# A graph attention layer: comparing edges with places and nodes on TensorE and ScalarE, loading sources by sixteens of rows, eight row buffers, and the 0/1 matrix and q in float32

## The chip, the cores and the metric

The kernel runs on one core of a Trainium2 chip. The metric is the device time of one execution in microseconds (us). Ten executions of the kernel before gave a median of 2691.25 us, from 2687.83 to 2693.83.

A core has five engines that run their own instruction streams side by side and wait for each other by semaphores: PE (TensorE, matmuls; its weight loads are listed as PEld), DVE (VectorE), ACT (ScalarE), POOL (GpSimd) and SP (SyncE, which here only issues transfers). Matmul results lie in PSUM, in banks of 128 partitions by 512 float32 columns; everything else lies in SBUF, 128 partitions wide.

## The reference

A graph of N = 12500 nodes with D = 128 features and M = 200000 edges that are sorted by their target node `dst`. Each node keeps the 16 best of its incoming edges, by a score, and adds the softmax-weighted messages of these to itself:

```python
h = relu(layernorm(x))
Qv, Ku = h @ W_Q.T, h @ W_K.T
score = einsum('md,md->m', Qv[dst], Ku[src]) / sqrt(128) * exp(-edge_weight)
keep  = rank of the edge by score among those of its dst < 16
w     = where(keep, exp(score - max over dst), 0)
alpha = w / (sum of w over dst)
agg   = segment_sum(alpha[:, None] * (h[src] @ W_msg.T), dst)
out   = x + relu(h @ W_self.T + agg)
```

Inputs and output are float32, indices int32.

## The kernel before

**Windows and chunks.** The edges are cut into chunks of 128 (one edge per partition), and 14 chunks (`GC`) make a window; there are G = 112 windows. A window's nodes are those whose edges begin in it, at most 128, one per partition; since the last of them can go on in the next window, a window works on 15 chunks (`NJ`), the fifteenth being the first of its neighbour.

**What is done for a window g**, by the names of the stages, with the engine and the line of the main instruction:

- `load_nodes`: SP loads the features of the nodes, `h_r` (from the table `h_tab` of normed rows, written in the setup) and `x_t`. `load_dst` (SP, L186): the targets of the window's 1920 edges, copied to all 128 partitions as int32, `dstb`, 960 KB.
- `let_go` (L464): DVE copies two chunks' source indices into `ix` (L472), and POOL issues an indirect gather for each of them (L172): 128 rows of `h_tab`, 64 KB, into `hs`. `hs` holds a window's 14 chunks and has seven buffers. 14 gathers a window.
- `h_turned`, `q_made`, `q_out`: the node rows transposed, and the queries q = hT times a_qk (W_Q and W_K in one matrix). `q_parts` (DVE, L516) splits the float32 q into three bfloat16 parts, whose sum is q.
- `far_of` (ACT, L522) and `to_edges` (ACT, L527): the 0/1 matrix of nodes by edges. Square of (dst minus the node's number) over 1920 columns, then Relu(1 - that): 1 where the edge belongs to the node, 0 elsewhere. Kept as bfloat16, `to_e`.
- `q_to_edges(g, b)` (PE, L546): each edge's own q, by a matmul of `to_e` with q, in four parts of four chunks, three matmuls a chunk (the three parts of q), into three banks of the tag "q". `scores` (DVE, L556): product with the gathered row, summed over the 128 features, and times the decay.
- `places` (DVE, L533 and L535): two more 0/1 matrices of 40 columns per chunk. `ow` says where in a strip of 40 nodes the edge's target stands (compared with `dlw`); `po` says the edge's place among its target's edges (compared with `pos_all`).
- `scores_in_slots` (DVE), `slots_by_node` (PE, L571, 15 matmuls into the bank "e"), `slots_out`, `node_by_slots`: the scores sorted into a matrix of nodes by 40 places.
- `best` (DVE, L585 to L597): the 16 best of 40, and `km`, which marks them. `sum_of_exps` (ACT, L602).
- `kept_to_edges` (PE, L614): the marks brought back to the edges, by `to_e`. `on_edges` (DVE, L620 to L627), `exps`, `weights` (DVE, L636): each edge's weight, laid out as a sparse matrix `alz`.
- `sums` (PE, L646, in two parts): `alz` times the gathered rows, summed over the 15 chunks in the one buffer of bank "a". `sums_out` (ACT, L651): times 1 over the sum, `agn`. After that `hs` of the window can be written again.
- `sums_turned`, `products`, `output`, `store`: the two weight matrices, relu, plus x, and the store.

**The order.** The loop (L684) is unrolled in full, as a software pipeline written by hand: iteration i runs each stage for another window, such as `q_to_edges` for i, `far_of` and `places` for i + 1, `slots_by_node` for i - 1, `best` and `kept_to_edges` for i - 2, `sums` for i - 3, `output` for i - 5, and `let_go` for i + 3 and i + 4 through `more(k)`. Each engine runs its instructions in the order of the program. Accesses to one PSUM bank wait for each other as whole banks: a new use of a bank with one buffer waits until its last reader is done.

**The setup** turns the index lists into columns: `src`, `dst` and the edge weights are loaded as 121 rows of 13 chunks (`RR`, `CPR`) on ACT's queue, and PE transposes them. `x` is loaded, normed and stored as `h_tab`. The first four windows (`RAW`) gather from `x` itself and are normed afterwards; the 42 gathers of windows 4 to 6 are issued together before the loop (`gather_at_once`). A general path behind a runtime flag follows the loop; it isn't taken here.

Of the kernel before, what the change touches and what calls it, by code (L numbers as in the profile page):

```python
# [20 lines left out]
P = 128  # L21
# [55 lines left out]
def gnn_layer(  # L77
# [38 lines left out]
    CPR = 13  # L116
# [4 lines left out]
    assert RR <= P and RR - RF <= 1  # L121
# [22 lines left out]
    nvec = const.tile([P, 1], F32, name="nvec")  # L144
    a_qk = const.tile([P, P], F32, name="a_qk")
    wselfT = const.tile([P, P], F32, name="wselfT")
    wmsgT = const.tile([P, P], F32, name="wmsgT")

    idx_all = const.tile([P, CW], I32, name="idx_all")
    dec_all = const.tile([P, CW], F32, name="dec_all")  # L150
    pos_all = const.tile([P, CW], F32, name="pos_all")
    dlw = const.tile([P, G, NJ], F32, name="dlw")

    nb = const.tile([P, G], F32, name="nb")
# [13 lines left out]
    def gather(g, j0, j1, index, table=h_tab):  # L168
        if j0 == 0:
            T[g]["hs"] = rows_pool.tile([P, GC, D], F32, name="hs", bufs=7)  # L170
# [8 lines left out]
    def load_dst(g):  # L179
        n = chunks[g] * P  # L180
        lo = g * EG
        T[g]["dstb"] = dstb = rows_pool.tile([P, NJ * P], I32, name="dstb", bufs=2)
        hi = min(lo + n, M)
        if hi < lo + n:
            nc.vector.memset(dstb[:, hi - lo:n], 1 << 21)
        nc.sync.dma_start(dstb[:, 0:hi - lo], dst[lo:hi].partition_broadcast(P))  # L186
# [47 lines left out]
    with tc.tile_pool(name="edges", bufs=1) as ep, ExitStack() as stage:  # L234
        prep = stage.enter_context(tc.tile_pool(name="prep", bufs=1))
        RL = HALO + RW

        src_r = ep.tile([RR, RL], I32, name="src_r")
        h0 = src_r.bitcast(F32)
        h1 = alz[0][0:RR, 0:RL]  # L240
        dst_all = alz[1][:, 0:CW]
        assert max(RL, CW) <= NJ * (WW + STEP)
        dst_r = ep.tile([RR, HALO + RW], I32, name="dst_r")
# [5 lines left out]

        def load_rows(t, a):  # L250
            if RF:
                nc.scalar.dma_start(t[0:RF, 0:RW], a[0:RF * RW].rearrange("(p c) -> p c", c=RW))
            if REM:
                nc.scalar.dma_start(t[RF:RF + 1, 0:REM], a[RF * RW:M].rearrange("(p c) -> p c", p=1))

        def to_columns(rows, lo, put):

            for j0 in range(0, CPR, 4):
# [5 lines left out]
                put(lambda t: t[:, 0:RR * CPR].rearrange("e (p j) -> e j p", j=CPR)[:, j0:j1, :],  # L264
# [3 lines left out]
        nc.vector.memset(src_r, 0)  # L268
        load_rows(src_r, src)
        xs, t = [], 0  # L270
        for i, n in enumerate(sizes):
            xg = prep.tile([HP, n, D], F32, name=f"xg{i}")
            for a, b in cuts:
                nc.sync.dma_start(xg[a:b], by_part(x)[a:b, t:t + n, :])
            xs.append((t, n, xg))
            t += n
        make_identity(nc, ident)
        nc.gpsimd.iota(dst_r, pattern=[[1, RL]], base=1 << 21, channel_multiplier=0)
        nc.gpsimd.memset(dst_r[0:1, 0:HALO], -1)
        nc.gpsimd.iota(slots, pattern=[[1, KM]], base=0, channel_multiplier=0,  # L280
# [3 lines left out]
        nc.vector.memset(ew_r, 0.0)  # L284
# [8 lines left out]
        nc.vector.memset(pos_all[:, RR * CPR:CW], 0.0)  # L293
        nc.vector.memset(dec_all[:, RR * CPR:CW], 0.0)
        nc.vector.memset(dst_all[:, RR * CPR:CW], float(1 << 21))
        for j in range(NJ):
            nc.vector.memset(w0[:, j:j + 1], float(lead(j)))
        for k in range(2):
# [6 lines left out]
        to_columns(src_f, 0, lambda at, p: nc.vector.tensor_copy(at(idx_all), p))  # L305
# [3 lines left out]
        def finish(i):  # L309
            t0, n, xg = xs[i]  # L310
            normed(xg, n, *stat[i])
            if i == 1:
                for t, w in zip(ws, (w_q, w_k, w_self, w_msg)):
                    nc.scalar.dma_start(t, w)
                nc.scalar.dma_start(b_i[:, 1:G],
                                    bass.AP(dst.tensor, dst.offset + EG - 1, [[EG, 1], [EG, G - 1]]))

                nc.scalar.dma_start(dst_r[0:1, HALO:], dst[0:RW].rearrange("(p c) -> p c", p=1))
                if RF > 1:
                    nc.scalar.dma_start(dst_r[1:RF, :], bass.AP(dst.tensor, dst.offset + RW - HALO,  # L320
                                                                [[RW, RF - 1], [1, RL]]))
# [608 lines left out]
```

## Time and profile before

| | |
|---|---|
| median of 10 runs | 2691.25 us (2687.83 to 2693.83) |
| the profiled execution | 2694.53 us |
| its span, first to last instruction | 2692.8 us |
| mean granted TensorE clock | 0.694 |
| setup, until the first `agn` | 215.1 us |
| last gather stream ends | about 2615 us |
| DMA moved | 253.17 MB, mean 94 GB/s |

Seen by stretches (busy us of each engine, instructions in brackets, the granted clock, the share of the DMA engines, and what they moved), the run is even from about 336 us on:

```profile
215.00:336.00 121.00, 75.50 (x666) 63.67 (x665) 73.66 (x337) 25.85 (x51) 72.76 (x70) 0.71 0.30 91
336.00:1000.00 664.00, 444.16 (x3772) 379.36 (x3772) 362.61 (x1860) 147.91 (x291) 389.67 (x406) 0.69 0.30 93
1000.00:2000.00 1000.00, 683.42 (x5686) 586.36 (x5686) 544.65 (x2786) 224.25 (x440) 587.72 (x612) 0.67 0.30 93
2600.00:2693.00 93.00, 60.38 (x626) 55.26 (x626) 54.52 (x265) 19.27 (x51) 13.34 (x13) 0.80 0.07 20
```

The order of the five engines is PE, PEld, DVE, ACT, POOL. A line of the profile such as `L646 PE MATMUL a<-hs,alz 128*128 128x128 f32 x1305 | 285.5, 386 | ...` is a group: line of the kernel, engine, operation, output and inputs by name, shapes, count, total busy us, mean ns of one, then the idle time of the engine just before these instructions and what ended it. A float32 matmul leaves two records. The ends of PE's records are modelled, and a wait whose releaser could not be found is called "remote".

### The profile page before, as it was taken

To read this page: it belongs to the slowest core of one execution; us is meant where nothing else is said; L and a number is where in the kernel's file an instruction comes from. 1 tells how busy PE (TensorE), PEld (TensorE's weight loads), DVE (VectorE), ACT (ScalarE), POOL (GpSimd) and SP (SyncE) were. 2 spreads that over 40 slices of the span, in tenths; PEclk is the share of its full clock that TensorE was granted. 3 is DMA by queue.
4 is the path that set the end of the run, shared out by engine and by line. 5 is a ranking of instruction groups with operands and counts; after the bars stand their busy time and mean duration, and the time that the engine had idled before them with its cause. 6 is when DMAs were issued, how large, how long until landed. Compare 5 with 4: busy or idle time off the path is not lost. (4 is left out here: it accounts for less than half of the span.)

```text
span 2692.8 us, 43581 instructions
## 1 busy us (share of the span) xinstructions
PE 1721.5 (64%) x14574; PEld 1474.3 (55%) x14575; DVE 1476.4 (55%) x7420; ACT 648.0 (24%) x1306; POOL 1522.1 (57%) x1578
## 2 busy tenths in 40 slices
PE   0226666666676666676666766666766666676676
PEld 0125555555565556565565655555655565555565
DVE  5447555555555555555555555555555555555555
ACT  5532122222222222222222222222222222222221
POOL 4734555555555555555555655555556555555540
PEclk9667666667767776766666666766677667766668
DMA  8412332333333333322332333233333333322320
GB/s 208 164 58 81 100 95 92 94 94 93 94 95 95 94 94 94 91 87 89 92 93 92 94 94 93 94 94 94 95 95 94 94 94 93 87 88 92 94 79 8
DMA packets 117573, 253.17 MB, mean 94 GB/s; under 512 B 32799, under 2 KB 76066, under 8 KB 116577
## 3 DMA queue, kind: packets, MB, share of 16 engines
q1 hardware_dynamic: 66104, 144.92, 15.5%
q0 software_dynamic: 50144, 102.74, 14.7%
q10 hardware_dynamic: 1094, 2.69, 0.5%
q8 instruction: 115, 1.88, 0.3%
q14 instruction: 116, 0.94, 0.1%
HBM read 236.40 MB, written 14.40 MB: 93 GB/s over the span
## 5 line engine op out<-in xcount | busy, mean ns | idle before, releaser
L172 POOL DMA_INDIRECT hs<-h_tab,ix x1465 | 1412.2, 964 | 1040.7 <-DVE prod L556 504.9
L646 PE MATMUL a<-hs,alz 128*128 128x128 f32 x3348 | 707.8, 377 | 98.9 <-issue 86.3
L546 PE MATMUL q<-q,to_e 128*128 128x128 bf16 x5022 | 546.1, 258 | 307.5 <-issue 257.9
L646 PEld LDWEIGHTS a<-hs,alz 128*128 128x128 f32 x3348 | 649.5, 283 | 147.3 <-issue 127.5
L546 PEld LDWEIGHTS <-to_e 128*128 128x128 bf16 x5022 | 418.2, 115 | 381.3 <-issue 368.9
L556 DVE SCALAR_TENSOR_TENSOR prod<-hs,dec_all,q 128x128 f32<-128x128 f32 x1674 | 483.7, 343 | 70.7 <-remote 53.9
L585 DVE TENSOR_SCALAR ell<-slots,e 128x40 f32<-128x40 f32 x112 | 27.9, 249 | 872.6 <-remote 841.3
L571 PE MATMUL e<-ow,sl 128*41 128x40 f32 x3348 | 250.8, 250 | 47.1 <-issue 45.3
L602 ACT ACTIVATE e<-v,km 128x16 f32<-128x16 f32 x112 | 34.4, 307 | 974.0 <-DVE km L594 964.9
L571 PEld LDWEIGHTS e<-ow,sl 128*41 128x41 f32 x3348 | 221.0, 166 | 71.9 <-issue 57.6
L654 PE MATMUL s<-ident,agn 128*128 128x128 f32 x112 | 40.4, 360 | 300.5 <-DVE o L666 99.2
L651 ACT ACTIVATE agn<-a,rden 128x128 f32<-128x128 f32 x112 | 41.1, 367 | 775.6 <-remote 550.7
L522 ACT ACTIVATE far<-dstb,nb 128x1920 bf16<-128x1920 int32 x112 | 213.0, 1901 | 0.0
L527 ACT ACTIVATE to_e<-far 128x1920 bf16<-128x1920 bf16 x112 | 201.1, 1796 | 0.0
L654 PEld LDWEIGHTS s<-ident,agn 128*128 128x128 f32 x112 | 17.5, 156 | 323.3 <-ACT agn L651 153.1
L556 DVE DVE_READ_ACCUMULATOR prod<-hs,dec_all,q 128x1 f32 x1674 | 138.0, 82 | 0.0
L472 DVE COPY ix<-idx_all 128x2 int32<-128x2 int32 (+1 forms) x733 | 130.6, 178 | 0.0
L666 DVE SCALAR_TENSOR_TENSOR o<-s,x_t 128x128 f32<-128x128 f32 x112 | 32.5, 290 | 126.0 <-issue 119.1
L614 PE MATMUL x<-km,to_e 128*128 128x43 bf16 x1674 | 78.8, 204 | 35.5 <-DVE km L597 30.9
L506 PE MATMUL s<-a_qk,hT 128*128 128x128 f32 x224 | 57.2, 337 | 68.0 <-ACT hT L503 57.8
L614 PEld LDWEIGHTS <-to_e 128*128 128x128 bf16 x1674 | 66.7, 112 | 58.9 <-DVE km L597 55.1
L564 DVE TENSOR_TENSOR sl<-po,s 128x600 f32<-128x600 f32 x112 | 87.6, 782 | 3.8
(166 smaller groups left out, 1639.3 us busy)
## 6 DMA issues: line engine op xcount, KB each, us to landing
dstb<-in_dst_dram SPq DMA_DIRECT2D x111, 960.0 KB
hs<-h_tab,ix POOLq DMA_INDIRECT x1465
h_r<-h_tab SPq DMA_DIRECT2D x112, 64.0 KB
x_t<-in_x_dram SPq DMA_DIRECT2D x108, 64.0 KB
out_dram<-o SPq DMA_DIRECT2D x108, 64.0 KB
xg<-in_x_dram SPq DMA_DIRECT2D x2, 1400.0 KB
h_tab<-xg SPq DMA_DIRECT2D x2, 1400.0 KB
xg<-in_x_dram SPq DMA_DIRECT2D x1, 1120.0 KB
```

The costliest lines, as they stand in the source:

```text
L172: nc.gpsimd.indirect_dma_start(out=T[g]["hs"][:, j, :], out_offset=None, in_=table[0:N, :], in_offset=bass.IndirectOffsetOnAxis(ap=index(j ...
L472: nc.vector.tensor_copy(ix[:, j0:j1], idx_all[:, GC * g + j0:GC * g + j1])
L506: nc.tensor.matmul(so[:, P:2 * P], lhsT=T[g]["hT"], rhs=a_qk, start=True, stop=True)
L522: nc.scalar.activation(T[g]["far"][:, 0:n], T[g]["dstb"][:, 0:n], AF.Square, bias=nb[:, g:g + 1])
L527: nc.scalar.activation(T[g]["to_e"][:, 0:n], T[g]["far"][:, 0:n], AF.Relu, bias=1.0, scale=-1.0)
L546: nc.tensor.matmul(pq[:, (j - j0) * P:(j - j0 + 1) * P], lhsT=T[g]["to_e"][:, j * P:(j + 1) * P], rhs=upper(T[g]["q"][:, k, :]), start=(k ...
L556: nc.vector.scalar_tensor_tensor(prod, rows_of(g, j), dec_all[:, c:c + 1], T[g]["pq", b][:, (j % 4) * P:(j % 4 + 1) * P], op0=OP.mult, op1 ...
L564: nc.vector.tensor_tensor(sl1[g % 2][:, 0:n, 0:KM], T[g]["po"][:, 0:n, :], bc(T[g]["s"][:, 0:n], KM), op=OP.mult)
L571: nc.tensor.matmul(et[0:KM + 1, STEP * j:STEP * j + WN], lhsT=sl1[g % 2][:, j, :], rhs=T[g]["ow"][:, j, :], start=False, stop=(j == n - 1))
L614: nc.tensor.matmul(px[:, j, 0:KM + 3], lhsT=T[g]["to_e"][:, j * P:(j + 1) * P], rhs=upper(T[g]["km"]), start=True, stop=True)
L646: nc.tensor.matmul(T[g]["pa"][:, 0:P], lhsT=alz[g % 2][:, WW * j + PRE:WW * j + PRE + P], rhs=rows_of(g, j), start=(j == 0), stop=(j == n ...
L654: nc.tensor.transpose(so[:, 2 * P:3 * P], T[g]["agn"], ident)
```

## The change

Five things are done together.

1. *Targets.* `load_dst` is gone. The setup keeps `rel`, 112 rows (one per window) of 1920 numbers in bfloat16: the edge's target minus the target of the edge just before the window's first, minus 1. `far_of` runs in four blocks of up to 512 edges: a matmul with a one-hot column copies the window's row of `rel` to all 128 partitions, in bank "a", and ACT squares it with the node's number subtracted.
2. *Places.* The two comparisons on DVE are gone. `edges_turned` transposes a window's 2 x 15 numbers per edge (`pd`: place and strip offset) by a matmul into bank "a", and ACT copies it to SBUF; `away`, three times, subtracts the 40 places by a matmul with the constant `minus_at`, 400 columns into bank "a", and ACT squares; `places` is one Relu(1 - that) over 1200 columns on ACT, giving `po` and `ow` in one tile.
3. *Float32.* `to_e` is float32, and q is used as it is: `q_parts` is gone, and `q_to_edges` makes one float32 matmul a chunk in place of three bfloat16 ones. `kept_to_edges` reads the upper halves of `to_e`.
4. *Gathers.* Eight `hs` buffers, seven `ix` buffers, and `more` lets go of windows i + 4 and i + 5; windows 4 to 6 are gathered by `let_go` too, the first of them in the setup and the others in the first iterations.
5. *Setup.* 112 rows of 14 chunks; the loads stand on SP's queue, and large ones are cut at a multiple of 16 rows.

Bank "a", with one buffer, now takes nine uses a window in place of one. In the order, `slots_by_node` is cut in three between the blocks of `far_of`, and `kept_to_edges` stands before the first part of `sums`. The core of the diff:

```diff
-            T[g]["hs"] = rows_pool.tile([P, GC, D], F32, name="hs", bufs=7)
+            T[g]["hs"] = rows_pool.tile([P, GC, D], F32, name="hs", bufs=8)
...
-    def load_dst(g):
-        n = chunks[g] * P
-        lo = g * EG
-        T[g]["dstb"] = dstb = rows_pool.tile([P, NJ * P], I32, name="dstb", bufs=2)
...
-        nc.sync.dma_start(dstb[:, 0:hi - lo], dst[lo:hi].partition_broadcast(P))
...
+        def sixteens(a, b):
+
+            m = b - (b - a) % 16
+            return [(p, q) for p, q in ((a, m), (m, b)) if p < q]
+
         def load_rows(t, a):
-            if RF:
-                nc.scalar.dma_start(t[0:RF, 0:RW], a[0:RF * RW].rearrange("(p c) -> p c", c=RW))
+            for p0, p1 in sixteens(0, RF):
+                nc.sync.dma_start(t[p0:p1, 0:RW], a[p0 * RW:p1 * RW].rearrange("(p c) -> p c", c=RW))
...
-        for g in range(RAW, min(7, G)):
-            gather_at_once(g, h_tab)
...
+        nc.vector.tensor_scalar(rel, dst_f[:, HALO:], dst_f[:, HALO - 1:HALO], 1.0, op0=OP.subtract, op1=OP.subtract)
...
-        def q_parts(g):
-
-            q = T[g]["q"]
-            for k in range(2):
-                nc.vector.tensor_sub(q[:, k + 1, :], q[:, k, :], upper(q[:, k, :]))
...
+        def far_of(g, b):
+            n0, n1 = 4 * P * b, min(4 * P * (b + 1), chunks[g] * P)
+            if n0 >= n1:
+                return
+            if b == 0:
+                T[g]["far"] = win.tile([P, NJ * P], BF16, name="far")
+            pr = bank("a", 1)
+            nc.tensor.matmul(pr[:, 0:n1 - n0], lhsT=upper(ident[0:RR, g:g + 1]).to_broadcast([RR, P]),
+                             rhs=rel[:, n0:n1], start=True, stop=True)
+            nc.scalar.activation(T[g]["far"][:, n0:n1], pr[:, 0:n1 - n0], AF.Square, bias=minus)
...
-            T[g]["to_e"] = win.tile([P, NJ * P], BF16, name="to_e", bufs=4)
+            T[g]["to_e"] = win.tile([P, NJ * P], F32, name="to_e", bufs=4)
...
+        def edges_turned(g):
+            pr = bank("a", 1)
+            nc.tensor.matmul(pr[0:32, 0:P], lhsT=pd[:, g, :, :].rearrange("e w j -> e (w j)"), rhs=upper(ident),
+                             start=True, stop=True)
+            T[g]["pdT"] = win.tile([32, P], BF16, name="pdT")
+            nc.scalar.copy(T[g]["pdT"], pr[0:32, 0:P])
+
+        def away(g, b):
+            if b == 0:
+                T[g]["aw"] = win.tile([P, 2 * NJ * KM], BF16, name="aw")
+            n0, n1 = 400 * b, 400 * b + 400
+            pr = bank("a", 1)
+            nc.tensor.matmul(pr[:, 0:400], lhsT=T[g]["pdT"],
+                             rhs=minus_at.rearrange("k w j s -> k (w j s)")[:, n0:n1], start=True, stop=True)
+            nc.scalar.activation(T[g]["aw"][:, n0:n1], pr[:, 0:400], AF.Square)
+
         def places(g):
...
+            T[g]["opo"] = win.tile([P, 2, NJ, KM], F32, name="opo", bufs=4)
+            nc.scalar.activation(T[g]["opo"].rearrange("e w j s -> e (w j s)"), T[g]["aw"], AF.Relu, bias=1.0,
+                                 scale=-1.0)
...
-                for k in range(3):
-                    nc.tensor.matmul(pq[:, (j - j0) * P:(j - j0 + 1) * P],
-                                     lhsT=T[g]["to_e"][:, j * P:(j + 1) * P], rhs=upper(T[g]["q"][:, k, :]),
-                                     start=(k == 0), stop=(k == 2))
+                nc.tensor.matmul(pq[:, (j - j0) * P:(j - j0 + 1) * P],
+                                 lhsT=T[g]["to_e"][:, j * P:(j + 1) * P], rhs=T[g]["q"], start=True, stop=True)
...
             def more(k):
 
-                g, k = (i + 3, k + 2) if k < 5 else (i + 4, k - 5)
-                if 7 <= g < G:
+                if i in (-1, 0, 1):
+                    g = i + 6
+                else:
+                    g, k = (i + 4, k + 2) if k < 5 else (i + 5, k - 5)
+                    if g < 8:
+                        return
+                if i >= -1 and g < G:
                     let_go(g, k)
 
             at(i, q_to_edges, 0)
+            at(i + 1, edges_turned)
             at(i - 5, output)
             at(i - 5, store)
             at(i - 3, weights)
             more(0)
             at(i - 4, sums_turned)
+            at(i + 1, far_of, 0)
             at(i - 4, sums_turned_out)
             at(i + 1, q_out)
             at(i, q_to_edges, 1)
-            at(i + 1, far_of)
-            at(i - 1, slots_by_node)
-            at(i + 1, places)
+            at(i + 1, far_of, 1)
+            at(i - 1, slots_by_node, 0)
+            at(i + 1, far_of, 2)
+            at(i - 1, slots_by_node, 1)
+            at(i + 1, far_of, 3)
+            at(i - 1, slots_by_node, 2)
+            at(i + 1, away, 0)
...
             at(i - 2, sum_of_exps)
             at(i - 1, slots_out)
             at(i, q_to_edges, 2)
+            at(i + 1, away, 1)
             at(i + 2, h_turned)
+            at(i + 1, away, 2)
             at(i, scores, 0)
             more(3)
             at(i + 1, to_edges)
-            at(i + 1, q_parts)
             at(i + 2, h_turned_out)
+            at(i - 2, kept_to_edges)
             at(i - 3, sums, 0)
-            at(i - 2, kept_to_edges)
...
             more(5)
+            at(i + 1, places)
```

## The prediction

> **What bounds the kernel now.** I read the engines' shares first, then the waits, then one window of the steady stretch in the timeline, then the durations by tile. No engine is full:
>
> ```profile
> PE 1721.5 (64%) x14574; PEld 1474.3 (55%) x14575; DVE 1476.4 (55%) x7420; ACT 648.0 (24%) x1306; POOL 1522.1 (57%) x1578
> ```
>
> so the bound is a loop of waits. The view of waits (engine, tile and line, what ended the wait: total us, times, longest) names it; about 110 windows are run:
>
> ```profile
> DVE ell L585 <- remote: 841.3, 98, 8.7
> ACT agn L651 <- remote: 550.7, 78, 7.3
> POOL hs L172 <- DVE prod L556: 504.9, 207, 54.7
> ...
> POOL hs L172 <- remote: 138.8, 84, 2.1
> ```
>
> "remote" is a releaser that the profile could not name. The timeline of one window (start, duration, instruction, idle before it) shows what it is:
>
> ```profile
> 1503.39 0.37 ACT L651 ACTIVATE agn<-a,rden 128x128 f32<-128x128 f32 x1 [7.03 <-remote]
> 1503.58 0.94 POOL L172 DMA_INDIRECT hs<-h_tab,ix  x1 [1.67 <-remote]
> 1504.11 0.84 PE L546 MATMUL q<-q,to_e 128*128 128x128 bf16 x12
> 1507.14 0.33 PE L571 MATMUL e<-ow,sl 128*41 128x40 f32 x4 [0.41 <-issue]
> 1512.53 0.94 POOL L172 DMA_INDIRECT hs<-h_tab,ix  x1 [0.30 <-issue]
> 1515.14 0.25 DVE L585 TENSOR_SCALAR ell<-slots,e 128x40 f32<-128x40 f32 x1 [8.65 <-remote]
> 1517.54 0.94 POOL L172 DMA_INDIRECT hs<-h_tab,ix  x1 [4.07 <-DVE prod L556]
> 1519.30 3.72 PE L646 MATMUL a<-hs,alz 128*128 128x128 f32 x16
> 1526.29 0.37 ACT L651 ACTIVATE agn<-a,rden 128x128 f32<-128x128 f32 x1 [7.11 <-PE q L546]
> 1526.48 0.94 POOL L172 DMA_INDIRECT hs<-h_tab,ix  x1 [1.74 <-remote]
> ```
>
> POOL issues a window's 14 gathers as a stream of eight (1503.58 to 1513.47) and one of six (1517.54 to 1524.74), one per 1.25 us within each. Alone that is 14 x 1.25 = 17.5 us. Between the streams stand gap A (4.07) and gap B (1.74), of which 0.3 each is the ordinary distance, so the period is 17.5 + 3.77 + 1.44 = 22.7; from agn to agn it is 22.9, and 22.83 over the 44 windows of 1000 to 2000 us. Gap A is POOL waiting for the index copies of DVE (L472), which stand behind ell. And ell waits for the slots matmuls L571, whose last record here ends at 1507.5, though DVE goes on only at 1515.14, 1.7 us after the last gather of the stream was issued. Gap B is the same with sums: the 16 matmuls of L646 end at 1523.0, agn starts at 1526.29 and frees POOL's next row buffer. I read this so: while gathers run one behind another, other engines see PE's results late, and what is still open is released when the stream ends. The end of the run supports it, where no gathers are left and agn follows every 11 to 13.5 us:
>
> ```profile
> 2619.48 0.37 ACT L651 ACTIVATE agn<-a,rden 128x128 f32<-128x128 f32 x1 [3.33 <-PE a L646]
> 2630.45 0.37 ACT L651 ACTIVATE agn<-a,rden 128x128 f32<-128x128 f32 x1 [1.68 <-PE a L646]
> ```
>
> So the time is 2694.53 us (this execution, span 2692.8) = 336 us of setup and ramp + 100 windows x 22.83 up to 2615 + a tail of about 80. The median of the runs, 2691.25, is 3 us lower.
>
> **The change, part by part.** Durations (lines of 1000 to 2000 us; total busy, mean ns):
>
> ```profile
> L546 PE MATMUL q<-q,to_e 128*128 128x128 bf16 x1968 | 217.9, 260 | 120.5 <-issue 102.7 <-DVE prod L556 16.9
> L522 ACT ACTIVATE far<-dstb,nb 128x1920 bf16<-128x1920 int32 x44 | 83.9, 1908 | 0.0
> L533 DVE TENSOR_TENSOR ow<-slots,dlw 128x600 f32<-128x600 f32 x44 | 33.9, 772 | 0.0
> L535 DVE TENSOR_TENSOR po<-slots,pos_all 128x600 f32<-128x600 f32 x44 | 33.9, 771 | 0.0
> L516 DVE TENSOR_TENSOR q<-q 128x128 f32<-128x128 f32 x88 | 25.4, 288 | 1.5
> L510 ACT COPY q<-s 128x128 f32<-128x128 f32 x44 | 12.0, 272 | 0.0
> ```
>
> *Taken off DVE:* places 772 + 771 and q_parts 2 x 288 = 2.1 us of a window's 12.2 (DVE's 544.65 us in those 1000, by 44.) Places lies at the start of the eight-stream, ahead of 8.65 us of waiting for ell; q_parts lies in the six-stream. Neither ends a gap: worth 0.
>
> *The dst broadcast,* 960 KB a window, goes; nothing waits for it (far starts with no idle time before it). Worth 0 by itself; the second rival prices what it may do to others.
>
> *far by blocks.* One Square of 1908 ns becomes four, each behind a matmul of 512 columns in bank a. From 272 ns at 128 columns to 1908 at 1920 the slope is 0.913 ns a column, so 512 columns take 272 + 384 x 0.913 = 620 ns. The matmul: twelve L546 records take 0.84 us at full clock and 1.49 at half in two neighbouring windows, some 57 and 107 ns per 128 columns, so 0.23 to 0.43 us. The hand-over PE to ACT outside a lag: aggT (L658) starts 0.66 us after its matmul ends (1503.98 + 0.30, 1504.94), which I halve between there and back: a turn costs about 0.62 + 0.35 + 0.35 = 1.3 us. The three away turns with 400 columns (520 ns) cost 1.2 each, the turned edges about 0.9, places' Relu of 1200 columns 272 + 1072 x 0.913 = 1.25 us. So ACT rises from 5.1 to some 9.2 us a window and PE's wide matmuls add 2 to 3.5 us; neither fills.
>
> What matters is the order. Bank a has one buffer, so edges_turned, four far blocks, three away blocks and the sums follow each other, PE to ACT to PE, and PE executes in order: the second part of slots stands behind far block 2, the third, whose end ell needs, behind block 3. In the eight-stream block 1 stands behind q(1)'s 8 f32 records, block 2 behind slots' first 10. If their signals come late as L571's do now, then when the stream ends PE has not yet been allowed to issue the rest. Left from there: none of the turns if all four get through in the stream (for that speaks aggT, released within 0.66 us inside a stream), at most all four, 4 x 1.3 = 5.2 us. I take one and a half turns, **1.95 us on gap A**, since two blocks stand behind ten or more f32 records each and only these. Queued behind ell on DVE are the index copies, and POOL waits for those: all of it lands on the gap.
>
> *kept_to_edges* moves ahead of sums part 0 and behind away 2, whose bank waits for away 1's Square, which stands on ACT behind sum_of_exps and slots_out. It starts now 0.4 us after km; then e, its accumulator and eT (0.31 + 0.19 + 0.24), a Square (0.52) and one hand-over (0.35) lie ahead of it: 1.4 us later. Behind it PE holds 16 to 30 records of sums, which until now ran partly before km. The lag of 3.3 us between sums' end and agn can swallow all of it, or none: 0 to 1.7 on gap B, taken at **0.7**, since half the lag is needed by any release at the stream's end.
>
> *q in f32.* 45 bf16 records (57 or 107 ns apart) become 30 f32 ones (107 or 213, from the spacing of L646): 2.6 to 4.8 us become 3.2 to 6.4. That lies in the streams, where PE has room: 0, with 1.6 us a window as the upper bound, if the streams leave no room. to_e is written as f32: its Relu (1.80 us for 1920 columns) is at 0.94 ns a column as the one from int32 is at 0.99, so 0 to 0.1, and nothing waits for it but the next window's q.
>
> *Eight row buffers, gathers a window further ahead:* the first gather of a group still reuses the buffer that sums of the same iteration frees. Worth 0.
>
> *Setup:* 42 gathers of windows 4 to 6 no longer stand together ahead of the loop; the first of the steady windows is reached 0 to 30 us earlier. DVE's wait for the sources is 14.6 us, that ends some us sooner or not at all. The loads that leave ACT's queue stand on SP's ahead of the h_tab stores, some 20 issues of 0.34 us: up to 7 us. I take **-15** (5 to 25 gained). Tail: four windows without gathers, 1.5 us longer each, +6.
>
> A rule speaks against bank a as a whole. In the Trainium skill, "Perfetto Trace Analysis" (Optimizing Tensor Performance, Matmuls) wants independent matmul groups to rotate through different PSUM banks, so that one group's evacuation lies beside the next group's matmuls; here eight groups share one. The row is aggT's: a hand-over inside a stream that took 0.66 us, while PE went on with q. If the rule held in full, all eight turns would be exposed, 0.9 + 4 x 1.3 + 3 x 1.2 = 9.7 us a window, and the sum would be near 3650; by the row nearly all of it fits beside other work, and the sum would be near that of no change.
>
> Sum: 22.83 + 1.95 + 0.7 = 25.5 us a window; 2694.5 + 100 x 2.65 - 15 + 6 = 2950, 3 less against the median: **2947, said as 2950.**
>
> **Rivals.**
> *1. The turns fit, and gap B closes.* The deeper order gives POOL a free buffer one group earlier than I see, and the lighter DVE copies earlier: the period loses the 1.44 of gap B. 2694 - 144 - 15 = 2535. Against it: buffer and sums moved together. Chance 0.14.
>
> *2. The hold on PE comes from the broadcast, not from the gathers.* For it: in the window above the load is issued at 1507.19 and moves up to 436 GB/s between about 1508 and 1512, and PE's "issue" gaps (0.42, 1.08, 1.00, 0.65 us) lie just there; the six-stream has no load and a lag of 3.3 instead of 7.6. Against it: a lag is left there. If so, ell ends inside the eight-stream once its release comes 3.77 us or more sooner, gap A is gone, 2694 - 377 - 15 = 2302; with gap B too, 2160. This is the mechanism on the other side: it decides as soon as what the load cost is more than the 1.95 that the turns add. Chance 0.22.
>
> *3. It doesn't do what it says:* the streams set the pace, turns and saved DVE work are hidden alike, and only setup is left: 2670 to 2695, half of it within 0.2%. Chance 0.06.
>
> **How the numbers follow.** Forecast 0.58. Its own range: 23.3 us a window (2740) to 28 (3200); both upper bounds together, 29.7, would be 3370. Over all cases 2290 to 3180 leaves out about half of rival 2 and the highest tenth of the forecast. Two runs of this kernel differ by some 0.2%, so that is what can be told from no change: faster 0.14 + 0.22 + 0.03 = 0.39, within 0.2% 0.03, slower 0.58.
>
> **What would show it.** In the changed profile ell's wait should stay above 8 us a window, POOL's waits behind DVE (505 us now) should rise by some 200, and after an eight-stream a Square of far should run before ell. If gap A is near 0.3 us, the step on the turns is wrong and rival 2 or 1 right; if PE's records are on the path with no gap, q in f32 was priced too low.

## The result and the profile after

The changed kernel took 2776.17 us (median of 8 runs, 2773.14 to 2781.86), the kernel before 2690.94 (28 runs). The ratio is 1.0321, with a 95% interval of 1.0312 to 1.033: slower, by 85 us where 259 were forecast. The profiled execution has a span of 2779.6 us. Ratios compare executions of the fast state alone, so that one can differ a little from the ratio of the medians beside it.

The experiments below were run in five further sets, each with the kernel before beside it. In two of these sets the kernel before itself took 2077 to 2078 us in place of 2691 to 2715, and in the one of them in which the changed kernel ran, it was 1.0% faster; so every ratio is within its set, and the sets are called *with gaps* and *without gaps*, after what the trace shows between the gather streams.

The engines of the changed kernel, and a steady stretch of it (PE, PEld, DVE, ACT, POOL, then granted clock, DMA share and GB/s):

```profile
PE 1958.4 (70%) x13800; PEld 1564.7 (56%) x13801; DVE 1286.2 (46%) x6998; ACT 1052.0 (38%) x2198; POOL 1496.4 (54%) x1580
```

```profile
1000.00:2000.00 1000.00, 742.28 (x5220) 595.55 (x5220) 457.41 (x2565) 371.31 (x767) 561.60 (x594) 0.73 0.19 48
```

All that was to leave an engine or a queue has left it: DVE 544.65 to 457.41 us, the traffic 93 to 48 GB/s. POOL does less in the same time (594 gathers where it did 612), so the windows are longer. The view of waits of the changed kernel:

```profile
DVE ell L613 <- PE e L599: 899.5, 101, 11.0
POOL hs L176 <- DVE prod L583: 462.0, 103, 6.2
ACT far L536 <- remote: 439.9, 99, 6.4
ACT agn L679 <- PE a L674: 417.1, 111, 11.0
POOL hs L176 <- PE a L674: 206.0, 96, 5.8
```

The loop of waits is the one of before, with its new line numbers: ell for the slots matmuls (8.9 us a time, 8.6 before), POOL for DVE behind ell, POOL for the sums. Only "far" is new, ACT waiting for a block's matmul. One window in the timeline:

```profile
1510.38 0.37 ACT L679 ACTIVATE agn<-a,rden 128x128 f32<-128x128 f32 x1 [4.73 <-PE a L674]
1510.57 0.94 POOL L176 DMA_INDIRECT hs<-h_tab,ix  x1 [1.97 <-PE a L674]
1512.81 0.69 ACT L536 ACTIVATE far<-a,minus 128x512 bf16<-128x512 f32 x1 [0.47 <-issue]
1514.07 0.69 ACT L536 ACTIVATE far<-a,minus 128x512 bf16<-128x512 f32 x1 [0.26 <-PE a L534]
1514.81 0.38 PE L534 MATMUL a<-rel,ident 112*128 112x512 bf16 x1 [0.21 <-ACT far L536]
1519.12 0.69 ACT L536 ACTIVATE far<-a,minus 128x512 bf16<-128x512 f32 x1 [4.36 <-remote]
1519.31 0.94 POOL L176 DMA_INDIRECT hs<-h_tab,ix  x1 [0.30 <-issue]
1519.86 0.48 PE L534 MATMUL a<-rel,ident 112*128 112x384 bf16 x1 [4.16 <-ACT far L536]
1522.01 0.58 ACT L536 ACTIVATE far<-a,minus 128x384 bf16<-128x384 f32 x1 [2.20 <-PE e L599]
1522.12 0.25 DVE L613 TENSOR_SCALAR ell<-slots,e 128x40 f32<-128x40 f32 x1 [9.05 <-PE e L599]
1524.52 0.94 POOL L176 DMA_INDIRECT hs<-h_tab,ix  x1 [4.27 <-DVE prod L583]
```

Blocks 0 and 1 of far start within 4 us of the stream's start. Block 2's matmul is issued at 1514.81 and its Square starts only at 1519.12, 5.05 us after the one before it. Block 3's Square follows when the stream's last gather (1519.31) is done, and ell 0.1 us after it, 1.87 us behind that gather's end; before the change that distance was 1.67 (1513.47 to 1515.14).

This window is one kind of two. I count, for the streams of eight gathers between 336 and 2580 us, how many Squares of far start only after the last gather has ended:

| kernel | Squares left | streams | gap A | of it: last gather's end to ell | ell to the next gather |
|---|---|---|---|---|---|
| before (no blocks) | | 96 | 4.05 | 1.65 | 2.39 |
| changed | 1 | 48 | 4.26 | 1.86 | 2.39 |
| changed | 2 | 43 | 4.93 | 2.54 | 2.39 |

(Two more streams had none left.) On average 1.44 Squares are left.

Three stretches of the timelines tell where the 85 us went. The mean distance from agn to agn between 336 and 2580 us rises from 22.87 to 23.52 us; over the 96 windows between agn 4 and agn 100 that makes some 62. The first agn comes at 234.7 in place of 215.1 us: 19.6 more. From agn 100 to the last it is 173.2 in place of 166.7: 6.5 more. The first four windows lie 1.5 closer. Together 86.5, and the spans differ by 86.8 (2779.6 - 2692.8).

### The profile page after: what moved, and what is told of

Its sections match the earlier page's. It is cut to its first block, busy times and chain, and to the rows that moved or that the text cites. A ratio compares the mean times of both kernels' runs of the same rounds, so it can differ in the third digit from the quotient of the medians.

```text
span 2779.6 us, 42100 instructions
## 1 busy us (share of the span) xinstructions
PE 1958.4 (70%) x13800; PEld 1564.7 (56%) x13801; DVE 1286.2 (46%) x6998; ACT 1052.0 (38%) x2198; POOL 1496.4 (54%) x1580
## 3 DMA queue, kind: packets, MB, share of 16 engines
q0 software_dynamic: 50144, 102.74, 14.5%
HBM read 126.79 MB, written 14.40 MB: 51 GB/s over the span
## 5 line engine op out<-in xcount | busy, mean ns | idle before, releaser
L176 POOL DMA_INDIRECT hs<-h_tab,ix x1507 | 1431.2, 950 | 1154.9 <-DVE prod L583 462.0
L574 PEld LDWEIGHTS q<-q,to_e 128*128 128x128 f32 x3348 | 555.5, 246 | 181.0 <-issue 170.3
L574 PE MATMUL q<-q,to_e 128*128 128x128 f32 x3348 | 605.1, 337 | 0.3 <-issue 0.3
L536 ACT ACTIVATE far<-a,minus 128x512 bf16<-128x512 f32 (+1 forms) x447 | 294.9, 660 | 732.9 <-remote 439.9
L534 PE MATMUL a<-rel,ident 112*128 112x512 bf16 (+1 forms) x447 | 181.6, 406 | 506.7 <-ACT far L536 450.0
L599 PEld LDWEIGHTS e<-opo,sl 128*41 128x41 f32 x3348 | 187.1, 139 | 552.2 <-issue 543.3
L557 PE MATMUL a<-minus_at,pdT 32*128 32x400 bf16 x336 | 162.1, 482 | 154.7 <-ACT far L536 65.6
L559 ACT ACTIVATE aw<-a 128x400 bf16<-128x400 f32 x336 | 168.9, 503 | 257.1 <-PE a L557 224.0
L599 PE MATMUL e<-opo,sl 128*41 128x40 f32 x3348 | 228.9, 229 | 0.0
L541 ACT ACTIVATE to_e<-far 128x1920 f32<-128x1920 bf16 x112 | 200.4, 1790 | 0.0
L642 PEld LDWEIGHTS <-to_e 128*128 128x128 bf16 x1674 | 66.9, 114 | 99.2 <-DVE prod L583 62.8
```

What stands on the lines that cost most here:

```text
L176: nc.gpsimd.indirect_dma_start(out=T[g]["hs"][:, j, :], out_offset=None, in_=table[0:N, :], in_offset=bass.IndirectOffsetOnAxis(ap=index(j ...
L534: nc.tensor.matmul(pr[:, 0:n1 - n0], lhsT=upper(ident[0:RR, g:g + 1]).to_broadcast([RR, P]), rhs=rel[:, n0:n1], start=True, stop=True)
L536: nc.scalar.activation(T[g]["far"][:, n0:n1], pr[:, 0:n1 - n0], AF.Square, bias=minus)
L541: nc.scalar.activation(T[g]["to_e"][:, 0:n], T[g]["far"][:, 0:n], AF.Relu, bias=1.0, scale=-1.0)
L557: nc.tensor.matmul(pr[:, 0:400], lhsT=T[g]["pdT"], rhs=minus_at.rearrange("k w j s -> k (w j s)")[:, n0:n1], start=True, stop=True)
L559: nc.scalar.activation(T[g]["aw"][:, n0:n1], pr[:, 0:400], AF.Square)
```

## The experiments

For each kernel I give, where it has gaps, the means over all gaps of the timeline: gap A is the one behind ell, gap B the one that ends with agn. I call it a *hold* when other engines go on late while gathers run one behind another.

**1. Do the gathers hold the others up?** Both kernels, with the row gathers of windows 4 on replaced by plain loads of other rows on SP's queue. The set has gaps (before: 2714.59).

```diff
         for j in range(j0, j1):
+            if table is h_tab:
+                r0 = P * ((GC * g + j) % (N // P))
+                nc.sync.dma_start(out=T[g]["hs"][:, j, :], in_=h_tab[r0:r0 + P, :])
+                continue
             nc.gpsimd.indirect_dma_start(
```

> The kernel before, with the row gathers of windows 4 on replaced by plain loads of 128 consecutive rows on SP's queue (so the rows are other rows, and the output is not the layer's). Theory 1, that POOL's back-to-back gathers hold up the other engines: ell's wait (8.65 us a window) goes, the period falls from 22.9 to 12 to 16 us as in the last windows, time 1500 to 2000. Theory 2, that the chain over PE, DVE and ACT itself is the bound: the period stays above 20 us, time above 2450.

> The changed kernel with the same replacement. Theory 1: the period falls from 23.5 us to that of the hand-overs in bank a and PE's records, 16 to 19 us, time 1950 to 2250; the difference to the kernel before with plain loads (2 to 5 us a window) is the price of the change without gathers, larger than the 0.64 us with them. Theory 2: above 21 us, and the difference stays near 0.6.

Measured, one execution each: 1683.62 and 1832.27 us; 13.40 and 14.40 us from agn to agn. The wait of ell in the first and in the second (the view of waits):

```profile
DVE ell L589 <- PE e L575: 109.4, 108, 2.6
```

```profile
DVE ell L617 <- PE e L603: 419.9, 111, 5.4
```

In the first it is 1.0 us a time in place of 8.6, though the same rows of features, the same matmuls and the dst broadcast are all still there, at 156 GB/s in place of 93. So what holds ell in this set is POOL's gathers, and neither the chain over the engines nor the traffic. (That gathers alone aren't enough for it, part 4 shows.) Without them the change costs 1.0 us a window, less than the 2 to 5 that I expected. That is a net figure: ell waits 3.8 us a time in the second kernel, 2.8 more, while DVE, which is 86% busy in the first, has 1.8 us a window less to do (1449.0 and 1247.0 us over 112 windows).

**2. Wider spacing.** A memset on POOL after every gather of the loop, 128 columns in the kernel before, 64 in the changed one; same set.

```diff
                 in_offset=bass.IndirectOffsetOnAxis(ap=index(j), axis=0))
+            if table is h_tab:
+                nc.gpsimd.memset(spare, 0.0)
```

> The kernel before, with one memset of 128 columns on POOL after each gather of windows 4 on, so that gathers lie about 1.5 us apart in place of 1.25. Theory 1: the other engines are no longer held up, the gaps of 4.07 and 1.74 us shrink, and the period is about 14 x 1.5 = 21 us plus what is left of the gaps: 2450 to 2700 us, not slower than before. Theory 2: 14 x 0.25 us is added to each window: 3000 to 3090 us.

> The changed kernel with one memset of 64 columns on POOL after each gather. Theory 1: as in the kernel before, 2500 to 2760 us. Theory 2: 3050 to 3180 us.

Measured: 2738.6 us (1.0098, 1.0078 to 1.0117) and 2901.18 (1.0686, 1.0668 to 1.0704). The memset fills the 0.30 us that lie between two gathers anyway, so the spacing became 1.33 and 1.28 us and not 1.5. In the kernel before the gaps shrink from 5.77 to 4.61 us a window while 14 x 0.08 = 1.1 us are added; that fits a hold that eases with distance, but at this step it proves nothing. In the changed kernel the gaps did not shrink. Both times lie between the two theories' ranges. Inconclusive.

**3. Half of the gathers, and the first look without gaps.** Four kernels in one set, and in this set the kernel before took 2078.21 us. The first, every second gather replaced:

```diff
+            if table is h_tab and j % 2 and g >= 7:
+                r0 = P * ((GC * g + j) % (N // P))
+                nc.sync.dma_start(out=T[g]["hs"][:, j, :], in_=h_tab[r0:r0 + P, :])
+                continue
```

> The kernel before, with every second gather of windows 7 on replaced by a plain load of 128 consecutive rows on SP's queue (other rows, so the output is not the layer's). POOL's part falls from 17.5 to 8.75 us a window. Theory 1, a hold that comes with the length of a gather stream: streams of four and three gathers (5 and 3.75 us) hold little, the period is 14 to 17 us, 1800 to 2100 us in all. Theory 1b, each gather holds the others as long as it runs, whatever the length: the hold is about halved, 17.5 to 19.5 us a window, 2150 to 2350.

Measured: 1677.07 us, 13.43 us a window, as without any gather. Since the set has no hold, it can't tell the two forms of theory 1 apart; it gives the same 13.4 for the period of the other engines, with DVE 87% busy.

The second moves the index copies ahead of ell; the third and fourth undo a part of the change each:

```diff
             more(1)
-            at(i - 2, best)
             more(2)
+            more(3)
+            at(i - 2, best)
...
-            more(3)
```

```diff
-            T[g]["to_e"] = win.tile([P, NJ * P], F32, name="to_e", bufs=4)
+            T[g]["to_e"] = win.tile([P, NJ * P], BF16, name="to_e", bufs=4)
...
-                                 lhsT=T[g]["to_e"][:, j * P:(j + 1) * P], rhs=T[g]["q"], start=True, stop=True)
+                for k in range(3):
...
+                                     lhsT=T[g]["to_e"][:, j * P:(j + 1) * P], rhs=upper(T[g]["q"][:, k, :]),
...
             at(i + 1, to_edges)
+            at(i + 1, q_parts)
```

```diff
         def places(g):
...
+            nc.vector.tensor_tensor(T[g]["opo"][:, 1, 0:n, :], bm(slots, n), bc(dlw[:, g, 0:n], WN), op=OP.is_equal)
+            nc.vector.tensor_tensor(T[g]["opo"][:, 0, 0:n, :], bm(slots, n), bc(pd[:, g, 0, 0:n], KM), op=OP.is_equal)
...
-            at(i + 1, edges_turned)
...
-            at(i + 1, away, 0)
+            at(i + 1, places)
...
-            at(i + 1, away, 1)
-            at(i + 1, away, 2)
```

> The kernel before with the index copies of more(2) and more(3) placed ahead of best on DVE, so that gap A no longer stands between the streams. If gap A is POOL's time lost to the order of DVE, the period falls by up to 3.77 us: 2310 to 2450 us. If the gaps are where the other engines catch up with what the streams held back, the lost time only moves to gap B: 2650 to 2800.

> The changed kernel with q in three bfloat16 parts and to_e in bfloat16 again. If q in float32 costs nothing, as predicted: 2765 to 2790 us. If its matmuls, held during the streams, are the 0.64 us a window: 2700 to 2720. It may also be slower, since the split puts 0.58 us a window back on DVE: up to 2840.

> The changed kernel with both comparisons of places on DVE again, in float32 (no edges_turned, no away): bank a has five uses a window in place of nine, and DVE has 1.54 us more. If the turns in bank a are the 0.64 us a window, near half of it comes back: 2735 to 2755. If they lie beside other waits: 2765 to 2790; if DVE's load matters more: 2800 to 2900.

Measured: 2078.8 (1.0004, 0.9992 to 1.0017), 2056.7 (0.9897, 0.9869 to 0.9924) and 2066.38 (0.9947, 0.9922 to 0.9971). In none of these three traces is there a gap over 0.8 us from 200 us on; POOL sets the pace. What these edits do with gaps, this set can't tell; parts 5 and 6 repeat them.

**4. The changed kernel itself without gaps, and its loads.** The next set again had none (before: 2077.42). The last kernel puts the loads back on ACT's queue:

```diff
-            return [(p, q) for p, q in ((a, m), (m, b)) if p < q]
+            return [(a, b)]
...
-                nc.sync.dma_start(t[p0:p1, 0:RW], a[p0 * RW:p1 * RW].rearrange("(p c) -> p c", c=RW))
+                nc.scalar.dma_start(t[p0:p1, 0:RW], a[p0 * RW:p1 * RW].rearrange("(p c) -> p c", c=RW))
...
             normed(xg, n, *stat[i])
+            if i == 1:
+                for t, w in zip(ws, (w_q, w_k, w_self, w_msg)):
+                    nc.scalar.dma_start(t, w)
...
```

> The changed kernel, unchanged, beside the kernel before on the chip of this set. Where the kernel before takes about 2700 us (gaps between the gather streams): 2770 to 2800. Where it takes about 2080 (no gaps, POOL issues a gather every 1.25 us throughout): theory 1 says that the time is then the gathers' own, 1563 x 1.2475 = 1950 us plus start, stops and tail, so the loop costs nothing more than before and the earlier first gather (15.75 in place of 24.5 us) and the missing pause of POOL after the setup show: 2040 to 2090. Theory 2, that the turns in bank a lengthen each window anywhere: 2130 to 2200.

> The changed kernel with q in three bfloat16 parts and to_e in bfloat16 again, beside the changed kernel on the same chip. With gaps between the streams: if float32 costs nothing, within 10 us of the changed kernel; if its matmuls are what the streams hold back, 50 to 70 us less. Without gaps: within 10 us of it.

> The changed kernel with the comparisons of places on DVE again, beside the changed kernel on the same chip. With gaps: if the turns in bank a are the extra 0.64 us a window, 25 to 40 us less than it; else within 10. Without gaps: within 15 us of it.

> The changed kernel with its loads on ACT's queue again, in one piece each, those of the weights, dst and edge weights after the second group of rows is normed, as in the kernel before. The first gather starts 8 to 9 us later. With gaps: if the early and unbroken stream of raw gathers is what slowed ACT and DVE between 45 and 90 us, the first agn comes 10 to 20 us earlier than at 234.7 and the time falls by as much; else it rises by about 9. Without gaps: about 9 us more than the changed kernel.

| kernel | us | ratio (95%) | first agn | last gather ends |
|---|---|---|---|---|
| changed | 2057.31 | 0.9901 (0.9885 to 0.9918) | 178.4 | 2010.8 |
| q in bfloat16 parts | 2058.35 | 0.9904 (0.9888 to 0.9921) | 178.9 | 2010.4 |
| places on DVE | 2065.07 | 0.994 (0.9923 to 0.9957) | 157.8 | 2016.1 |
| loads as before | 2084.1 | 1.0031 (1.002 to 1.0042) | 204.5 | 2036.6 |

The engines of the changed kernel and its waits in this set:

```profile
PE 1651.8 (80%) x13800; PEld 1322.3 (64%) x13801; DVE 1273.4 (62%) x6998; ACT 1043.3 (51%) x2198; POOL 1511.3 (74%) x1580
```

```profile
DVE ell L613 <- PE e L599: 439.2, 104, 6.2
POOL hs L176 <- issue: 325.0, 1060, 2.1
```

POOL's largest wait is the 0.3 us between two gathers; its waits for DVE or PE have gone. The time is then the gathers' own: 1563 x 1.2475 = 1950 us, from 15.8 to 2010.8 with 45 us of pauses, and a tail of 44. The same gathers run in both kinds of set, and their packets take the same time (14.5% of 2779.6 us and 19.7% of 2055.1, both some 404 us); but here ell waits 4.2 us a time, near the 3.8 of part 1 without gathers. What the change brings here is the start: with the loads as before it loses 27 us, where I expected 9, and is 0.3% slower than the kernel before. The first agn at 178.4 and 157.8 shows the turns for the places in the first windows, but here POOL has run ahead by then and nothing of it reaches the end.

**5. With gaps again.** What the order on DVE is worth, and the float32 and the places undone together (before: 2694.22):

> The kernel before with the index copies of more(2) and more(3) ahead of best, beside the kernel before. Where that takes about 2700 us: if gap A is time that POOL loses to the order of DVE, 2310 to 2450; if the gaps are where the other engines catch up, 2650 to 2800. Where it takes about 2080: the same as it, as measured once.

> The changed kernel with q in three bfloat16 parts and the places on DVE again; far by blocks, the deeper gathers and the setup stay. Where the kernel before takes about 2700 us: if float32 and the four turns for the places are the loop's extra 0.64 us a window, 1.005 to 1.012 times the kernel before (the setup's 20 us remain); if they cost nothing, 1.03 as the changed kernel; if DVE's 2.1 us more matter, up to 1.06. Where it takes about 2080: within 0.985 to 1.0.

The first took 2835.0 us (four executions, 2804.78 to 2846.97; 1.0463, 1.0405 to 1.0521), more than either expectation gave: copies that come earlier make the kernel slower. Its waits:

```profile
DVE ell L585 <- remote: 1066.5, 96, 13.4
POOL hs L172 <- DVE rden L608: 530.3, 99, 7.3
```

The stream goes on past ell, and ell waits 11.1 us where it waited 8.6; POOL's gaps add up to 7.21 us a window in place of 5.77. So gap A isn't time that POOL loses to DVE's order. I read it as the time in which the others catch up; with a longer stream more is left to catch up.

The second took 2712.42 us (1.0071, 1.0054 to 1.0087), with gaps of 3.72 and 1.90 us and the first agn at 213.2. It keeps far by blocks, the new setup and the deeper gathers, and loses 0.7%, as expected if float32 and the places are what costs, where the whole change loses 3.2 to 5.5%.

**6. Which of the two** (before: 2712.88):

> The changed kernel, unchanged, as the measure for the three others: 1.03 times the kernel before where that takes about 2700 us, 0.99 where it takes about 2080.

> The changed kernel with q in three bfloat16 parts again. With gaps: if float32 is the loss, 2710 to 2725 with the first agn near 213 us; if the turns for the places are, 2765 to 2790 with the first agn near 235.

> The changed kernel with the places on DVE again. With gaps: if the turns in bank a are the loss, 2710 to 2730 with the first agn near 213 us; if float32 is, 2765 to 2800.

> The changed kernel with its loads on ACT's queue, late and in one piece, as in the kernel before. With gaps: if the early unbroken raw gathers cost the setup, the first agn at 215 to 225 and 10 to 20 us less than the changed kernel; if the setup's loss is in the hand-overs of the first windows, the first agn at 240 or later and 5 to 30 us more.

| kernel | us | ratio (95%) | first agn | agn to agn | gap A | gap B |
|---|---|---|---|---|---|---|
| before (first profile) | 2691.25 | | 215.1 | 22.87 | 4.09 | 1.70 |
| changed (first profile) | 2776.17 | 1.0321 | 234.7 | 23.52 | 4.43 | 2.12 |
| changed, this set | 2864.01 | 1.055 (1.0523 to 1.0578) | 228.0 | 24.36 | 5.34 | 2.06 |
| q in bfloat16 parts | 2962.23 | 1.0917 (1.0896 to 1.0938) | 234.3 | 25.29 | 6.33 | 2.03 |
| places on DVE | 2728.25 | 1.0065 (1.0042 to 1.0088) | 213.5 | 23.27 | 3.86 | 2.00 |
| loads as before | 2892.96 | 1.0653 (1.0619 to 1.0687) | 262.1 | 24.35 | 5.29 | 2.06 |

For the places the first of the two expectations came. For the float32 neither did: undoing it makes the kernel 98 us *slower*. The timeline of that kernel shows where (ACT's far blocks, then POOL):

```profile
1504.35 0.69 ACT L542 ACTIVATE far<-a,minus 128x512 bf16<-128x512 f32 x1 [0.46 <-PE a L540]
1510.83 0.69 ACT L542 ACTIVATE far<-a,minus 128x512 bf16<-128x512 f32 x1 [5.47 <-remote]
1513.77 0.69 ACT L542 ACTIVATE far<-a,minus 128x512 bf16<-128x512 f32 x1 [2.26 <-PE e L607]
1515.03 0.58 ACT L542 ACTIVATE far<-a,minus 128x384 bf16<-128x384 f32 x1 [0.56 <-PE a L540]
1518.27 0.95 POOL L176 DMA_INDIRECT hs<-h_tab,ix  x1 [6.35 <-DVE prod L591]
```

With twelve bfloat16 matmuls of q(1) ahead of block 1, in place of eight float32 records, block 1 comes 6.5 us after block 0 and not 1.3. Two blocks are left when the stream ends, and gap A is 6.35. The changed kernel has two left as well in 77 of 92 streams of this set; but there block 1 starts 4.3 us after the stream's start (median) and not 8.6, and block 2 at 10.8 and not 11.6, where the last gather ends at 9.7. The split's 0.58 us on DVE isn't the loss: with the places back on DVE it cost nothing that shows (1.0071 with it in part 5, 1.0065 without). With the places on DVE, only the last block is late:

```profile
1501.52 0.69 ACT L536 ACTIVATE far<-a,minus 128x512 bf16<-128x512 f32 x1 [1.12 <-issue]
1502.80 0.69 ACT L536 ACTIVATE far<-a,minus 128x512 bf16<-128x512 f32 x1 [0.59 <-PE a L534]
1507.08 0.58 ACT L536 ACTIVATE far<-a,minus 128x384 bf16<-128x384 f32 x1 [3.59 <-PE s L513]
...
1510.97 0.94 POOL L176 DMA_INDIRECT hs<-h_tab,ix  x1 [3.86 <-DVE prod L568]
```

Without edges_turned ahead of the blocks and away behind them, block 2 starts 5.9 us after the stream's start (median of 96), no Square is left at the last gather's end in 88 of 96 streams, and gap A is 3.86, shorter than in the kernel before. The places on PE and ACT (four turns and a Relu of 1200 columns) are the loss: 136 of the 151 us of this set. They cost in the setup too: the first agn is at 213.5 with the places on DVE and at 228.0 with the turns, while the loads, put back, cost 34 us there.

## Why the prediction was wrong

**The mechanism** was right where there are gaps: the streams hold up PE's results, the turns in bank a are caught in them, and what is left of them when the stream ends lands on gap A, through ell and the index copies. Two of the signs that I named for it came: ell's wait over 8 us, and a Square of far between the stream's end and ell. In the table of the first section the way from ell to the next gather is 2.39 us in every row, so what delays ell does land on the gap in full. The third sign did not come: POOL's waits behind DVE, 504.9 us before, were to rise by some 200 and are 462.0.

**Gap A, "one and a half turns, 1.95 us"**, is the term that failed. It measured 0.34 us (4.43 - 4.09) in the run that counts, and 1.25 (5.34 - 4.09, against the first profile) in another set. The number of turns was right: on average 1.44 Squares are left when the stream ends (1.84 in the set of part 6, so one and a half was near and partly luck). Wrong was the step that priced each of them in full, at 1.3 us behind the stream. With no block at all ell comes 1.65 us after the last gather's end. One turn left fits into that nearly whole: ell comes at 1.86 and gap A is 0.21 longer; with two left, 0.88 longer. In the set of part 6 two are left in most streams (77 of 92), and there gap A is 5.59, 1.54 longer than in the profile before the change. So the price of a turn isn't fixed either; it depends on how late block 2 is released, and what sets that stays open.

**Gap B, 0.7**: 0.42 (2.12 - 1.70). The size is near, but the reason that I gave, kept_to_edges behind away 2, isn't shown: without any away block gap B is still 2.00. The windows' length, 0.64 more in place of 2.65, is near the sum of both gaps.

**The setup, -15**, has the wrong sign: +19.6. The gain that I priced is there, and larger: the loads by sixteens and early are worth 26.8 us without gaps and 29 in the whole with them. But I left the first windows out: they make the same turns, and in the set of part 6 those for the places put the first agn from 213.5 to 228.0. That isn't all. With the loads put back the first agn is at 262.1, 47 us after that of the kernel before (215.1), and the turns for the places are 14.5 of these; the rest belongs to what is left of the change (far by blocks, the gathers of windows 4 to 6 in the loop, the setup's new tables) and wasn't told apart.

**The tail, +6**, was 6.5, partly by luck: I had four windows without gathers 1.5 us longer each, and in the trace the gathers end a window earlier and the windows behind them differ by -2 to +4 us. **q in float32, 0**: right without gaps (2057 against 2058); with gaps it is a gain of 0.93 us a window as long as the turns are there (25.29 - 24.36); that fewer instructions then stand before block 1 is my explanation, argued and not tested. Without those turns it is none that shows: 1.0071 without float32 in one set, 1.0065 with it in another. My price by the spacing of records answered the wrong question. **Eight row buffers and the deeper order, 0**: the first gather behind gap B follows agn in both traces, as said; not tried alone. **The saved 2.1 us of DVE, 0**: with the places (1.54 us of it) back on DVE gap A got shorter, so nothing waited for it. Two sums of mine were off, and nothing hangs on them: DVE's 544.65 us over 44 windows are 12.4 a window and not 12.2, and ACT's terms add up to some 8.7 and not 9.2 (measured: 371.31 over 42.5 windows, 8.7).

**The rivals.** The second, that the broadcast holds PE up, falls: it is gone and ell waits as long; and with it kept and the gathers gone (the first experiment) ell waits 1.0 us. The first falls as well, gap B grew, and the third with the 62 us in the loop. Rule and row on the banks, set against each other in the prediction: with all eight turns exposed the period would have risen by 9.7 us; it rose by 0.64, and by 1.0, net of DVE's lighter work, with no gathers at all. What the Trainium skill asks for in "Perfetto Trace Analysis" (Optimizing Tensor Performance, Matmuls), another bank for each independent group, wasn't tried.

**On the other side.** Without gaps the change is a gain of 20 us, and the part that brings it is the early loads. The kernel with the places on DVE and the rest of the change comes nearest to serving both, 1.0065 with gaps and 0.994 without; no version here beats both kernels in both.

## What to carry to other kernels

When one engine's stream holds up the signals of the others, count the hand-overs that stand inside it before pricing busy time: four short turns between PE and ACT cost more here than 1.5 us of DVE work that nobody waited for. Then price what is left at the stream's end against the delay that is there already: the first turn here fitted into 1.65 us that ell waited anyway, and only the second showed. A gap of the busiest engine can be the time in which the others catch up; closing it by reordering made this kernel 4.6% slower.

## What the runs showed of the hardware that I had not expected

**One kernel, two times.** The kernel before took 2691 to 2715 us in four sets and 2077 to 2078 in two, with the same program. In the second kind (traces of the changed kernel and of the kernel before with its copies moved) POOL's gathers follow each other without gaps and ell's wait falls, from 8.9 to 4.2 us a time in the changed kernel. What decides it stays open. The kernel isn't it, and the chip alone isn't either: the sets of parts 1 and 4 ran on the same chip, one with gaps and one without.

**What the hold may count.** In the changed kernel's setup, raw gathers run for some 70 us with no pause over 1 us. ACT's norming of x in the first profile, and the same line in the set without gaps:

```profile
52.84 0.49 ACT L220 ACTIVATE xg<-xg,smx,rsx 125x128 f32<-125x128 f32 x1 [0.90 <-issue]
54.24 0.49 ACT L220 ACTIVATE xg<-xg,smx,rsx 125x128 f32<-125x128 f32 x1 [0.91 <-issue]
55.65 0.49 ACT L220 ACTIVATE xg<-xg,smx,rsx 125x128 f32<-125x128 f32 x1 [0.91 <-issue]
```

```profile
45.67 9.72 ACT L220 ACTIVATE xg<-xg,smx,rsx 125x128 f32<-125x128 f32 x25 [0.60 <-DVE smx L218]
```

There is one instruction every 1.40 us, waiting for nothing that the profile shows, where the same one takes 9.72 / 25 = 0.39 us. DVE's statistics come at 0.70 or 1.40 us from 47 to 51 us. The granted TensorE clock is 1.00 from 47 to 68 us in both profiles, so a throttled clock isn't the reason. Before the change DVE shows a cadence of 0.70 us too, from 40.8 us on:

```profile
41.51 0.29 DVE L194 BATCH_NORM_STATS2 stx<-xg 125x6 f32<-125x128 f32 x1 [0.40 <-issue]
42.21 0.29 DVE L194 BATCH_NORM_STATS2 stx<-xg 125x6 f32<-125x128 f32 x1 [0.40 <-issue]
```

It ends at 45.7, 2.6 us into a pause of POOL; ACT keeps to its 0.39 us in that time, so not every engine is held at once. That twelve small bfloat16 matmuls were caught longer than eight float32 records fits with it: what is held seems to be the instruction and not its work. This last step is argued from these rows and wasn't tested by itself.
